# Another order for the opening of a paged-attention kernel: second tile's projections, key-head copies and one batch's values

## Chip, cores and metric

The kernel runs on one core of a Trainium2 chip. The metric is the time of one execution on the device in microseconds (us). The profile is of one further execution, taken by the hardware profiler. The core has five engines with an instruction stream each: TensorE (PE; its weight loads are shown apart as PEld), VectorE (DVE), ScalarE (ACT), GpSimd (POOL) and SyncE (SP), which here only issues transfers. An engine takes its instructions in order and waits at semaphores.

## What is computed

64 sequences of 32 tokens with 512 channels go through two residual layers, in float32. The first adds a 32 x 32 mix of the tokens that the sequence's condition picks. The second is grouped-query attention with 32 query and 8 key heads of 128 channels, over 512 cached positions (masked beyond the sequence's length) and the 32 new ones, with normed and rotated queries and keys, and an output projection.

```python
x = x + einsum('bct,bcd->bdt', x, weights[condition])
q = rope(rmsnorm(x @ Wq.T), pos)
k = rope(rmsnorm(x @ Wk.T), pos)
v = x @ Wv.T
k_all = concat(k_cache[block_table], k)
v_all = concat(v_cache[block_table], v)
o = softmax(mask(q @ k_all.T * scale)) @ v_all
x = x + o @ Wo.T
```

## The kernel before

**Tiles and steps.** Four sequences (batches, 4 x 32 = 128 tokens) make a tile; there are 16 tiles. Each is passed twice, once for each half of the key heads (four key heads, sixteen query heads), which gives 32 steps. A step has 16 slots: four batches by four score groups. A slot makes one group's scores and exponentials (`scores`, L1027 and L1038) and one earlier group's values (`values`, L1090, with its division on DVE, L1101 to L1104). Further work is put into slots by hand, among it the next tile's projections (`plan`, filled through `at`).

**A tile's input.** `x1_a` loads x. `x1_c` mixes tokens with one product against a block-diagonal matrix `bds` (L408) and adds on DVE (L409). `x1_b` transposes the result on PE (L416), and ACT copies it to `x1t` (L421). `q_a` and `k_a` project (L470, four products of 512 columns, eight rows in the trace), and `finish` squares on ACT (L479), takes the root on POOL (L487, L488), and norms and rotates on DVE (L496 to L514). The tile of the squares is also one of the rotation's two. `q_b` and `k_b` (`to_columns`) transpose the rows on PE (L527), and ACT copies them into `q_ring` (L612). PE's products for all of these share four PSUM banks in rotation ("pp").

**Cached keys and values.** `load_half` issues eight transfers of 64 KB on SP for half a batch's keys (`k_t`, three buffers); `head_keys` copies two heads of one half into `kh` (L1016 on ACT, L1018 on DVE; four buffers). For score group j the half is j // 2 and the heads are those of j % 2. `fetch` gathers 128 value rows with an indirect transfer from POOL (L354; three buffers) and `fill` copies them, masked, into `v_ring` (L366).

**The opening.** The first 130 lines or so of the main part (from `first, second = steps[0:2]`) are written out in the order in which each engine takes them, with no slots: the first tile's whole input, its projections, batch 0 and the beginning of batch 1, and of the second tile the mix and the key projection. In the list below, PE's order there, the second tile is marked with a 2:

mix, transposes, queries 0, keys, queries 1, queries 2, rows of queries 0 and keys, values of the new tokens, rows of queries 1, scores (0,0), mix 2, scores (0,2), values (0,0), queries 3, rows of queries 2, transposes 2, keys 2, rows of queries 3, scores (0,1), (0,3), new scores, scores (1,0), new values. Queries 0 to 3 of the second tile stand in slots 4 to 7 of step 0.

**SP's order there.** x, condition weights (`w_all`), query weights 0 and 1, keys of batch 0, value weights, x of tile 2, four blocks of condition weights for tile 2 (L288), query weights 3, keys of batch 1 (first half), the second half, six parts of the output weights (`wo`), keys of batch 2, x of tile 3, its four blocks, six more parts of `wo`, keys of batch 3, and so on. SP and ACT share eight semaphores for their transfers, so that an issue waits for the landing of an earlier transfer with its semaphore. Key weights and query weights 2 are issued by POOL.

**Sines.** Angles are reduced on DVE (`reduced`, seven operations) and their sines taken on ACT, for two tiles at a time; `rot_tables` makes a tile's rotation tables on POOL and DVE. A table load on ACT (L1278) readies the exponential.

## Time and profile before

| what | us |
|---|---|
| runs shown (3): lowest, median, highest | 2072.66, 2073.85, 2074.44 |
| profiled execution, its own time | 2073.99 |
| its span | 2072.1 |
| PE busy, of the span | 2044.2 |
| DVE busy | 1629.5 |
| POOL busy | 1002.9 |
| ACT busy | 958.4 |
| PE busy in the first 63 us | 52.60 |
| mean granted PE clock, whole span | 0.997 |

The span runs from the program's first instruction to its last; the execution's own time has 1.9 us more around it. Rows of the profile give an engine, a source line, the operation and the tiles it writes and reads (out<-in), the partitions by elements, how often, and the time; an idle time before is given with what ended it. An "L" with a number is a line of the kernel before.

### The profile page before, as it was taken

To read this page: it belongs to the slowest core of one execution; us is meant where nothing else is said; L and a number is where in the kernel's file an instruction comes from. 1 tells how busy PE (TensorE), PEld (TensorE's weight loads), DVE (VectorE), ACT (ScalarE), POOL (GpSimd) and SP (SyncE) were. 2 spreads that over 40 slices of the span, in tenths; PEclk is the share of its full clock that TensorE was granted. 3 is DMA by queue.
4 is the path that set the end of the run, shared out by engine and by line. 5 is a ranking of instruction groups with operands and counts; after the bars stand their busy time and mean duration, and the time that the engine had idled before them with its cause. 6 is when DMAs were issued, how large, how long until landed. Compare 5 with 4: busy or idle time off the path is not lost.

```text
span 2072.1 us, 45314 instructions
## 1 busy us (share of the span) xinstructions
PE 2044.2 (99%) x13460; PEld 1596.7 (77%) x13460; DVE 1629.5 (79%) x3533; ACT 958.4 (46%) x2707; POOL 1002.9 (48%) x1138
## 2 busy tenths in 40 slices
PE   8999999999999999999999999999999999999998
PEld 4767667787887878778786677878878788787897
DVE  4555687988969789697996769879797887979854
ACT  4444354444545444454434445344454445445351
POOL 4354465645636455363544445445363544536351
PEclk9999999999999999999999999999999999999999
DMA  8767557667676666787767876676767667676682
GB/s 244 198 183 223 154 153 233 184 196 217 180 219 191 210 201 189 212 265 223 217 190 208 233 207 195 196 206 180 213 182 216 185 193 210 184 211 180 191 233 75
DMA packets 410144, 413.33 MB, mean 199 GB/s; under 512 B 58944, under 2 KB 325824, under 8 KB 409888
## 3 DMA queue, kind: packets, MB, share of 16 engines
q1 hardware_dynamic: 353472, 228.55, 38.3%
q0 software_dynamic: 55680, 181.58, 28.7%
q8 instruction: 109, 1.79, 0.4%
q14 instruction: 147, 1.20, 0.2%
q10 hardware_dynamic: 736, 0.21, 0.0%
HBM read 350.09 MB, written 60.03 MB: 198 GB/s over the span
## 4 chain that ended last, share of the span: by engine, by line
PE 79%; DVE 7%; DMA 6%; SPq 3%; issue 3%; POOL 2%; ACT 1%; DVEq 0%; POOLq 0%; ACTq 0%
PE ps_x L1027 18%; PE po_x L1090 17%; PE p_x L837 13%; PE pb_x L698 8%; PE pc_x L698 6%; PE pa_x L698 5%; PE pout_x L794 3%; DMA k_t_x<-in_kt_dram 3%; SPq L321 2%; PE pnv_x L1072 2%; PE pp_q_x L470 2%; PE psn_x L1048 1%; DMA raw_x<-in_vc_dram,v_row 1%; PE pp_v_x L470 1%; DVE kh_x L1018 1%
## 5 line engine op out<-in xcount | busy, mean ns | idle before, releaser
L354 POOL DMA_INDIRECT raw_x<-in_vc_dram,v_row x512 | 550.7, 1076 | 626.7 <-ACT v_ring_x L366 513.2
L1038 ACT ACTIVATE pr_x<-ps_x 128x512 f32<-128x512 f32 x511 | 305.4, 598 | 777.5 <-PE ps_x L1027 772.4
L1090 PEld LDWEIGHTS po_x<-v_ring_x,pr_x 128*128 128x128 f32 x4088 | 523.5, 192 | 85.4 <-issue 67.3
L1027 PE MATMUL ps_x<-q_ring_x,kh_x 128*128 128x128 f32 x4088 | 547.7, 277 | 1.6 <-ACT q_ring_x L612 1.6
L1090 PE MATMUL po_x<-v_ring_x,pr_x 128*128 128x129 f32 x4088 | 544.1, 276 | 2.2 <-DVE nv_x L1101 2.2
L1027 PEld LDWEIGHTS ps_x<-q_ring_x,kh_x 128*128 128x128 f32 x4088 | 499.7, 192 | 13.9 <-issue 3.3
L366 ACT ACTIVATE v_ring_x<-raw_x,valid 128x512 f32<-128x512 f32 x512 | 342.9, 713 | 21.9 <-DMA raw_x<-in_vc_dram,v_row 21.5
L1018 DVE COPY kh_x<-k_t_x 128x512 f32<-128x512 f32 x506 | 218.6, 432 | 97.3 <-PE ps_x L1027 68.2
L544 POOL DMA_DIRECT2D heads_d<-rows_x x150 | 125.8, 839 | 278.0 <-DVE rows_x L540 211.1
L698 PE MATMUL pb_x<-t_x,early 128*128 128x512 f32 x504 | 238.4, 596 | 2.6 <-DVE t_x L726 1.2
L1101 DVE TENSOR_TENSOR nv_x<-po_x,nv_x 128x258 f32<-128x258 f32 x256 | 106.8, 417 | 101.3 <-PE po_x L1090 96.6
L837 PEld LDWEIGHTS p_x<-wo_x,ot_x 128*128 128x128 f32 x624 | 116.8, 190 | 62.1 <-issue 45.8
L488 POOL TENSOR_TENSOR rs_q_x<-ms_q_x,minus_half 128x4 f32<-128x4 f32 x128 | 158.7, 1240 | 10.7
L837 PE MATMUL p_x<-wo_x,ot_x 128*128 128x256 f32 x624 | 156.4, 380 | 0.1
L837 PE MATMUL p_x<-ts_x,ot_x 128*128 128x256 f32 x624 | 145.5, 380 | 0.0
L698 PEld LDWEIGHTS pb_x<-t_x,early 128*128 128x128 f32 x504 | 86.2, 191 | 65.4 <-issue 60.6
L837 PEld LDWEIGHTS p_x<-ts_x,ot_x 128*128 128x128 f32 x624 | 115.6, 191 | 24.2 <-issue 8.4
L1104 DVE TENSOR_TENSOR nv_x<-nv_x,rden 128x256 f32<-128x256 f32 x256 | 109.5, 428 | 8.7
L479 ACT ACTIVATE sq_q_x<-u_x 128x128 f32<-128x128 f32 x224 | 66.3, 298 | 93.9 <-DVE u_x L714 93.9
L698 PE MATMUL pc_x<-wq_x,early 128*128 128x512 f32 x224 | 105.4, 593 | 0.0
L698 PE MATMUL pa_x<-wq_x,early 128*128 128x512 f32 x224 | 105.4, 593 | 0.0
L514 DVE TENSOR_TENSOR rope_q_x<-rope_q_x,rs_q_x 128x512 f32<-128x512 f32 x120 | 82.2, 685 | 19.7 <-POOL rs_q_x L488 19.3
(207 smaller groups left out, 2629.6 us busy)
## 6 DMA issues: line engine op xcount, KB each, us to landing
k_t_x<-in_kt_dram SPq DMA_DIRECT2D x2048, 64.0 KB
heads_d<-rows_x POOLq DMA_DIRECT2D x150, 256.0 KB
q_ring_x<-heads_d SPq DMA_DIRECT2D x464, 80.0 KB
raw_x<-in_vc_dram,v_row POOLq DMA_INDIRECT x512
wo_x<-in_wo_dram SPq DMA_DIRECT2D x32, 256.0 KB
res_x<-acc_d SPq DMA_DIRECT2D x31, 256.0 KB
wq_x<-in_wq_dram SPq DMA_DIRECT2D x8, 512.0 KB
early<-x1t_d SPq DMA_DIRECT2D x16, 256.0 KB
```

Source lines behind the costliest of these rows:

```text
L354: nc.gpsimd.indirect_dma_start(out=raw.rearrange("p g d -> p (g d)"), out_offset=None, in_=vc, in_offset=bass.IndirectOffsetOnAxis(ap=v_ro ...
L366: nc.scalar.activation(v_ring[:, c, :, 0:D], raw, AF.Copy, scale=valid[:, b, c : c + 1])
L488: nc.gpsimd.tensor_tensor(rs, ms, minus_half, ALU.pow)
L544: nc.gpsimd.dma_start(heads_d[st.n][:, :, i, :].rearrange("k p c -> p k c"), part)
L698: nc.tensor.matmul(bank, pair.x[:, i, c, :], by[:, c * 512 : (c + 1) * 512], start=start and c == 0, stop=c == 1, skip_group_check=not start,)
L837: nc.tensor.matmul(to, left[:, i, :], right(i), start=start and i == 0, stop=i == QH // 2 - 1, skip_group_check=True,)
L1018: nc.vector.tensor_copy(to, src)
L1027: nc.tensor.matmul(ps[:, c, i, :], ba.k[j][:, i, c, :], queries(ba, g + i), start=True, stop=True,)
L1038: nc.scalar.activation(pr, ps, AF.Exp, scale=SCALE)
L1090: nc.tensor.matmul(ba.po[g][:, i, :], ba.pr[j][:, c, i, :], ba.v_t[:, 2 * half + c, g + i, :], start=(half == 0 and c == 0 and i == 0), st ...
L1101: nc.vector.tensor_tensor(t, ba.po[g], t, ALU.add)
L1104: nc.vector.tensor_tensor(t[:, :, 0:D], t[:, :, 0:D], rd.unsqueeze(2).to_broadcast([P, 2, D]), ALU.mult,)
```

## The change

In the opening:

- the second tile's x is loaded between query weights 0 and 1, and its block-diagonal matrix is filled from `w_all` by DVE, as the first tile's is, in place of four transfers;
- its mix stands behind the first query projection, its transposes behind the second, its tables and the write of its x behind the third; `x1t` of the second tile lies in another buffer ("acc") than the first's;
- its key projection and query projections 0 and 1 move: keys and queries 0 before the values of the new tokens, queries 1 behind the first tile's queries 3 (queries 0 and 1 were in slots 4 and 5);
- the angles and sines of tiles 2 and 3 come behind the second tile's key projection, with the exponential's table load, in another buffer ("nv");
- batch 0's key heads are copied in the order 0, 1, 2, 3: two behind the second tile's key projection, two behind its queries 0;
- the values of batch 0, group 0, stand behind the rows of the first tile's queries 3.

PE's order is then: mix, transposes, queries 0, mix 2, keys, queries 1, transposes 2, queries 2, rows of queries 0 and keys, keys 2, rows of queries 1, queries 0 of 2, values of the new tokens, scores (0,0), (0,2), queries 3, rows of queries 2, queries 1 of 2, rows of queries 3, values (0,0), scores (0,1), (0,3), new scores, scores (1,0), new values. SP no longer issues the four blocks; x of tile 2 comes earlier; the rest keeps its order.

```diff
@@ x1_b
             if st.pair is None:
+                tag = "x1t" if exact else "acc" if st.n == 1 else "u3"
...
+                    tag=tag,
+                    bufs=2 if tag == "acc" else 1,
@@ opening
         load_w("q", 0, 0)
+        x1_a(second)
         load_w("q", 0, 1)
...
         load_w("v", 0)
-        x1_a(second)
...
+        def pick_weights(t):
+            number = conditions(t, mybir.EngineType.DVE)
+            for i in range(BT):
+                blk = slice(i * S, (i + 1) * S)
+                nc.vector.tensor_copy(
+                    bds[t][blk, blk],
+                    w_all[:, bass.ds(number[i], 1), :].rearrange("p o e -> p (o e)"),
+                )
+
+        pick_weights(0)
...
-        load_cond_weights(1)
         load_w("q", 0, 3)
         later = Batch(first, 1)
         later.load_half()
+        pick_weights(1)
...
-        trig = work.tile([P, 3, TRIG * HD], F32, tag="w1", name="trig1", bufs=1)
-        reduced(TRIG, trig)
-        q_a(first, 0)
-        sines(new_trig(TRIG), trig)
-        table = small.tile([P, 1], F32, tag="rs", name="table")
-        nc.scalar.activation(table, half_pi, AF.Exp)
+        pp = project(first, wt["q", 0, 0], "pp_q_first")
+        x1_c(second)
+        finish(first, 0, pp, f"q_{first.name}_0", "q")
...
-        q_a(first, 1)
+        pp = project(first, wt["q", 0, 1], "pp_q_first_1")
+        x1_b(second)
+        finish(first, 1, pp, f"q_{first.name}_1", "q")
+        trig = work.tile([P, 3, TRIG * HD], F32, tag="nv", name="trig1", bufs=1)
         q_a(first, 2)
         fetch(0, RAW, tag="pn", bufs=1)
+        keep_x1(second, nc.gpsimd)
+        rot_tables(second)
         q_b(first, 0)
-        head_keys(batch, 0, nc.scalar)
-        head_keys(batch, 2, nc.scalar)
         k_b(first)
-        head_keys(batch, 1, nc.scalar)
+        k_a(second)
+        for j in (0, 1):
+            head_keys(batch, j, nc.scalar)
+        reduced(TRIG, trig)
+        q_b(first, 1)
+        q_a(second, 0)
+        for j in (2, 3):
+            head_keys(batch, j, nc.scalar)
+        sines(new_trig(TRIG), trig)
+        table = small.tile([P, 1], F32, tag="rs", name="table")
+        nc.scalar.activation(table, half_pi, AF.Exp)
         later.load_half()
-        head_keys(batch, 3, nc.scalar)
...
         new = v_product(first)
-        q_b(first, 1)
         scores(batch, 0)
...
         v_copy(first, new)
-        x1_c(second)
...
         scores(batch, 2)
-        values(batch, 0)
         q_a(first, 3)
         q_b(first, 2)
-        x1_b(second)
-        keep_x1(second, nc.gpsimd)
+        q_a(second, 1)
         head_keys(later, 0, nc.scalar)
         head_keys(later, 1, nc.scalar)
         after.load_half()
-        rot_tables(second)
-        k_a(second)
         q_b(first, 3)
+        values(batch, 0)
         scores(batch, 1)
@@ slots of step 0
-        for g in range(GH):
+        for g in (2, 3):
             at(0, 4 + g, lambda g=g: q_a(second, g))
```

## The prediction

> **What bounds the kernel now.** I read the busy table first, then TensorE's order of time over the opening, then the granted clock by stretch, and last SP's order of time with its waits and one row of DVE.
>
> ```profile
> PE 2044.2 (99%) x13460; PEld 1596.7 (77%) x13460; DVE 1629.5 (79%) x3533; ACT 958.4 (46%) x2707; POOL 1002.9 (48%) x1138
> ```
>
> TensorE (PE) is busy for all but 27.9 us of the 2072.1 us span. The change adds no matrix work and takes none away, so it can only win back idle time and slowly clocked time. The order of time of PE shows where the opening holds these (start, duration, engine, line, operation; in brackets the idle time before, and who ended it):
>
> ```profile
> 27.69 0.60 PE L527 MATMUL pt_x<-ident,rows_x 128*128 128x128 f32 x4
> 29.37 0.63 PE L527 MATMUL pt_x<-ident,rows_x 128*128 128x128 f32 x4 [1.07 <-DVE rows_x L514]
> 32.78 6.30 PE L470 MATMUL pp_v_x<-wv_x,x1t_x 128*128 128x512 f32 x8 [2.79 <-DMA wv_x<-in_wv_dram]
> ...
> 40.19 0.94 PE L1027 MATMUL ps_x<-q_ring_x,kh_x 128*128 128x128 f32 x6 [0.45 <-ACT q_ring_x L612]
> ...
> 43.61 3.60 PE L470 MATMUL pp_q_x<-wq_x,x1t_x 128*128 128x512 f32 x8
> ...
> 49.54 3.70 PE L470 MATMUL pp_k_x<-wk_x,x1t_x 128*128 128x512 f32 x8 [1.45 <-ACT x1t_x L421]
> ...
> 55.08 0.94 PE L1027 MATMUL ps_x<-q_ring_x,kh_x 128*128 128x128 f32 x6 [1.18 <-ACT q_ring_x L612]
> ```
>
> Five waits: 1.07 + 2.79 + 0.45 + 1.45 + 1.18 = 6.94 us. The value projection also takes 6.30 us where the same eight matmuls take 3.60 us at 43.61. The windows say why (columns: stretch, PE, PEld, DVE, ACT, POOL busy, granted clock, DMA share, GB/s):
>
> ```profile
> 30.00:35.00 5.00, 2.22 (x3) 1.18 (x4) 3.58 (x8) 3.09 (x13) 4.58 (x6) 0.62 0.96 287
> 35.00:40.00 5.00, 4.74 (x12) 2.00 (x10) 1.69 (x4) 1.53 (x4) 1.12 (x1) 0.69 0.91 311
> 40.00:45.00 5.00, 4.81 (x28) 3.62 (x29) 0.83 (x2) 3.98 (x8) 1.92 (x2) 1.00 0.47 134
> ```
>
> The clock is halved from 31.25 to 38.08 us, after the wait for wv: 2.70 us lost. The ceiling of the change is thus 6.94 + 2.70 = 9.64 us.
>
> The second stream to watch is SP's, which issues the keys (k_t), the output weights (wo) and more, in one order:
>
> ```profile
> 24.75 0.51 SPq L264 DMA_DIRECT2D wv_x<-in_wv_dram  x1
> ...
> 43.94 3.30 SPq L262 DMA_DIRECT2D wo_x<-in_wo_dram  x6
> 48.52 15.49 SPq L321 DMA_DIRECT2D k_t_x<-in_kt_dram  x16
> ...
> 66.95 2.89 SPq L262 DMA_DIRECT2D wo_x<-in_wo_dram  x6
> ```
> ```profile
> SPq L321 <- DMA wo_x<-in_wo_dram: 10.1, 11, 1.9
> ```
> ```profile
> 95.17 0.43 DVE L1018 COPY kh_x<-k_t_x 128x512 f32<-128x512 f32 x1 [1.76 <-DMA k_t_x<-in_kt_dram]
> ```
>
> The second fence is from SP's wait list of 36 to 115 us (total, times, longest): key issues stood 10.1 us behind landings of wo, 11 times. The third is from DVE's order of time: at 93.41 it wanted the keys of batch 4 and waited 1.76 us. Nobody on PE felt it, but the keys were no longer early there.
>
> **The change, part by part.** Times of the changed kernel are estimates: its order of instructions, filled with the durations above.
>
> *Loads.* The second tile's x (256 KB) goes ahead of the second query weights; its four weight blocks (SP busy from 26.43 to 29.32) become four DVE copies from w_all. The same step for the first tile took 0.73 us for four copies, after at most 0.9 us for reading the numbers; DVE stands idle for 2.63 us at that place, until 13.48 (lens), so 1.6 us is hidden. Without that cover it would be 1.6 us. 256 KB more at the 380 GB/s of 10 to 16 us is 0.7 us on the queue: query weights 1 land at 20.9 instead of 20.22 (5.19 + 15.03 in the chain of waits), PE wants them at 21.7; each later key issue, and wv, go 0.7 us later (wv lands near 33.3; 24.75 + 7.89 in that chain before), and wq3, issued at 29.37 before, goes out near 26.3.
>
> *Mixing the second tile behind the first projection.* PE: 0.86 us; DVE's sum comes at 20.0, when the masks are done, where `reduced(TRIG)` (2.07 us, at 19.87) stood. That and the two sines and the table load on ACT no longer hold the first rope back: it starts at 20.75 instead of 23.00. From there ropes and squares alternate over one buffer (squares at 25.17, rope at 26.35, squares at 28.54): 3.36 us for each projection.
>
> *Key and query projection of the second tile before the value projection.* PE runs on without a wait: projection 13.73 to 17.39, mix 18.25, keys 21.70, queries-1 25.14, transposes 25.57, queries-2 29.0, two transposes 29.86, second tile's keys 33.3, one transpose 33.75, its queries-0 37.2, values 40.64 (wv is there since 33.3). 1.07, 2.79 and the slow clock are gone.
>
> *What comes next is late instead.* POOL has the second tile's tables (six operations, 1.69 us) behind the fourth fetch and the acc write: they end at 36.4. So the second key rope starts at 36.1, `reduced` ends at 41.05, the sines at 42.05, the table load (1.28) and its use at 43.55; behind these in ACT's order stands the first exponential (41.17 before). Then exponential, four fills, value copy, exponential (4.0 us, as 41.17 to 45.19) and the squares of queries-3: 47.65 to 48.8. Rope and rows end at 51.7, and PE, which has finished the second tile's queries-1 at 49.7, waits 2.05 us for them. After 0.45 + 0.85 + 0.39 us of work it waits another 0.5 us for the last query columns, behind two key copies on ACT. The scores that ran at 55.08 run at 53.95.
>
> *Key heads.* The order 0, 1, 2, 3 puts the copies at 34.9 to 36.1 and 39.4 to 40.6, against 33.39 to 36.08 before: later, not earlier. What it costs is the buffers' release; SP does not want the first before 37.4 nor the second before 46, so nothing.
>
> *Values of batch 0 behind the fourth query group.* 0.89 us that now fills part of that wait; no cost.
>
> *Slots 4 and 5.* Two projections less, 2 x 3.44 = 6.88 us. With 55.08 - 53.95 = 1.13 us, PE stands 8.0 us ahead there.
>
> *The cover that went.* The 6.88 us lay over the key loads. SP's stream does not gain 8 us: it hangs on landings. It is ahead by what wq3 does: key issues resume near 37.4 instead of 38.31, a further gain from the acc write leaving the wo stretch (256 KB, at some 200 GB/s 1.3 us), and a loss from two value fetches that now fall into the second wo stretch (0 to 2.6 us). I take 1.5 us; bounds 0 and 3.0. DVE takes batch 4's keys in order, and behind them the queue to the third tile's sum: from 95.17 to 103.98, less 2.42 us of waits for PE, is 6.4 us. So the transposes of L416, at 104.85 before, could have run at 101.7: the slack is 3.1 us. The gain there is 3.1 + 1.5 = 4.6 us, not 8.0 (bounds 3.1 and 6.1). Past 130 us SP waits for DVE again, and what is won stays.
>
> **Sum.** min(8.0, 4.6) = 4.6 us off the profiled execution's 2073.99 us: 2069.4; against the median 2073.85: 2069.25 us.
>
> *Rule against row.* The new 2.05 us wait lies in a 3.41 us window with 1.4 us of work in it, 41%; before, the clock fell after a window that PE filled to 32%, and, near 1168 us, to 64% with many 32-row products. So I count up to 1.7 us (one window at half clock) against PE's 8.0, which leaves 6.3 and does not touch the 4.6.
> The Trainium skill (TensorE: Matmul & The Clock Gate, "Part 1: The HAM clock gate") asks for an idle window of about 3.4 us before the clock drops; the trace disagrees, since 2.79 us of waiting was enough. By the rule PE would keep its 8.0 us.
>
> **Rivals.**
>
> *PE's path decides (22%).* SP keeps pace, since its keys are never late for PE itself in the profile. Gain 8.0, or 6.3 with the slow clock: 2065.9 to 2067.6. Against it: DVE's 1.76 us wait.
>
> *Keys not earlier at all, fetches in the way (15%).* Stream 1.1 us late (2.6 - 1.5): gain 2.0 us, 2071.9. For it: 66 to 80 us has a DMA share near 1 in the windows.
>
> *Slower (13%): slow clock in the thinned slots.* Without the two projections PE waits for keys in slots 8 to 15. Where more than 2.3 us of a 3.41 us window is waited, the clock halves as at 31.25 and costs 3.4 us (6.83 us at half). Two such falls on top of the former rival: 2.0 - 6.8 = 4.8 us lost, 2078.6. Against it: before, PE filled 67% of its worst window there (85.9 to 89.3) at full clock.
>
> *The change doesn't do what it says* holds for the key heads: they are not copied as they land. It costs nothing above, so it moves no number.
>
> **How the numbers follow.** Forecast 50% (2067.7 to 2070.8 from its bounds), rivals 22, 15 and 13. A measurement here can tell some 0.2%, 4.15 us, from no change: below 2069.7 is faster. Of the forecast's range about six tenths lie below that: 0.30 + 0.22 = 0.52 faster; 0.20 + 0.15 = 0.35 the same; 0.13 slower. The range for 8 in 10 goes from 2065.4 (PE's path) to 2073.5 (keys without gain, plus one window at half clock).
>
> **What would show it.** Right: no wait before pp_v and clock 1.00 from 14 us to 48; a PE wait of about 2 us on the fourth queries' rows near 50; a DVE wait for k_t of 5 us or more between 84 and 95, and PE's idle behind it. Wrong: no such DVE wait (then 8 us), or a wait of PE in the opening's first 40 us (wq1, wv or the ropes late), or PEclk below 1 between 80 and 105 us.

## The result and the profile after

The changed kernel takes 2069.15 us in the median of 22 runs (2064.80 to 2077.22), the kernel before 2074.18 us in as many on the same chips. The ratio is 0.9981, its 95% interval 0.9973 to 0.9989: 3.9 us less, somewhere from 2.3 to 5.6 (the medians alone lie 5.0 us apart). The profiled span is 2068.4 us against 2072.1.

From the page of the changed kernel, the busy times:

```profile
PE 2043.8 (99%) x13460; PEld 1596.8 (77%) x13460; DVE 1633.0 (79%) x3537; ACT 954.7 (46%) x2707; POOL 1003.6 (49%) x1138
```

TensorE idles for 24.6 us where it idled for 27.9, and its busy time is 0.4 us shorter. That nearly the same work was done with less waiting is all that these two numbers say; where the waits went, TensorE's order of time shows (start, duration, engine, line, operation, tiles; in brackets the idle time before and who ended it; lines are those of the changed kernel, where L470, L527, L1027 and L1090 have become L475, L532, L1032 and L1095):

```profile
36.34 3.60 PE L475 MATMUL pp_v_x<-wv_x,x1t_x 128*128 128x512 f32 x8
...
50.96 0.63 PE L532 MATMUL pt_x<-ident,rows_x 128*128 128x128 f32 x4 [1.92 <-DVE rows_x L519]
...
79.72 1.13 PE L1095 MATMUL po_x<-v_ring_x,pr_x 128*128 128x129 f32 x8 [2.56 <-DVE nv_x L1106]
80.69 1.80 PE L1032 MATMUL ps_x<-q_ring_x,kh_x 128*128 128x128 f32 x8
82.28 1.93 PE L1095 MATMUL po_x<-v_ring_x,pr_x 128*128 128x129 f32 x8
...
98.62 0.60 PE L416 MATMUL px1t_x<-ident,acc_x 128*128 128x128 f32 x4
```

The wait for wv is gone and the value projection takes 3.60 us (6.30 before). The opening's five waits are gone; a new one of 1.92 us, for the rows of the fourth queries, has come. And in slot 9 of the first step the wait is longer: 2.56 us at 79.72, where the kernel before waited 1.13 us at 87.58. The two groups behind it take 1.80 and 1.93 us where such a group takes 1.06. The kernel before, in the same order of time:

```profile
87.58 1.13 PE L1090 MATMUL po_x<-v_ring_x,pr_x 128*128 128x129 f32 x8 [1.13 <-DVE nv_x L1101]
...
104.85 0.60 PE L416 MATMUL px1t_x<-ident,acc_x 128*128 128x128 f32 x4
```

The windows of the changed kernel's profile (stretch, busy PE, PEld, DVE, ACT, POOL, granted clock, DMA share, GB/s) give the reason:

```profile
76.00:79.40 3.40, 1.16 (x11) 0.97 (x9) 2.94 (x7) 2.45 (x6) 2.92 (x4) 1.00 0.90 238
79.40:82.80 3.40, 3.08 (x19) 3.11 (x20) 2.78 (x10) 0.28 (x2) 1.78 (x2) 0.71 0.80 235
82.80:86.20 3.40, 3.40 (x26) 3.40 (x26) 2.07 (x6) 1.32 (x3) 0.00 (x0) 0.79 0.75 212
```

After the thin window the clock is half for 3.4 us, from 80.8 to 84.2. What TensorE waits for stands on DVE behind two rotations, these behind ScalarE's squares, and these behind a fill, in ScalarE's order of time:

```profile
63.62 0.75 ACT L366 ACTIVATE v_ring_x<-raw_x,valid 128x512 f32<-128x512 f32 x1
70.48 0.72 ACT L366 ACTIVATE v_ring_x<-raw_x,valid 128x512 f32<-128x512 f32 x1 [6.11 <-DMA raw_x<-in_vc_dram,v_row]
...
71.59 0.27 ACT L484 ACTIVATE sq_q_x<-pp_q_x 128x128 f32<-128x128 f32 x1
```

The projection whose squares start at 71.59 had ended on TensorE at 68.4: ScalarE stood still for 6.11 us at the fill ahead of them, whose gather had not landed. In the kernel before the same fill waited for nothing. GpSimd's issue of its gather there and, below it, in the changed kernel:

```profile
65.18 1.10 POOL L354 DMA_INDIRECT raw_x<-in_vc_dram,v_row  x1 [9.19 <-ACT v_ring_x L366]
```
```profile
62.95 1.31 POOL L354 DMA_INDIRECT raw_x<-in_vc_dram,v_row  x1 [10.24 <-ACT v_ring_x L366]
```

ScalarE's order of time in the kernel before:

```profile
67.38 0.28 ACT L479 ACTIVATE sq_q_x<-pp_q_x 128x128 f32<-128x128 f32 x1 [1.88 <-PE pp_q_x L470]
...
69.58 1.32 ACT L366 ACTIVATE v_ring_x<-raw_x,valid 128x512 f32<-128x512 f32 x2
```

There the squares of the projection in slot 4 stand ahead, and ScalarE comes to the fill, the second of that pair, near 70.2, some 5.0 us behind the issue of its gather. In the changed kernel it comes to it at 70.48 - 6.11 = 64.37, 1.4 us behind the issue.

And the keys, which the prediction takes for the limit? SP's order of time:

```profile
41.97 2.80 SPq L262 DMA_DIRECT2D wo_x<-in_wo_dram  x6
46.34 11.27 SPq L321 DMA_DIRECT2D k_t_x<-in_kt_dram  x16
57.79 0.34 SPq L396 DMA_DIRECT2D acc_x<-in_x_dram  x1
```

In this execution the third tile's x goes out at 57.79 us (64.13 before), and DVE's copies of keys never wait for a landing between 45 and 150 us.

A measure that a time of 2070 us with some 3 us of scatter (the standard deviation of the changed kernel's 22 runs is 3.3) can't drown is the **stretch** from the start of the first projection to the transposes of the third tile's mixed x (L416): 104.85 - 13.73 = 91.12 us before, 98.62 - 12.59 = 86.03 us after, 5.1 us less. To the fourth tile's transposes it is 158.25 and 153.47 us, 4.8 us less; to the end of the span it is 2072.1 - 13.73 = 2058.4 and 2068.4 - 12.59 = 2055.8 us, only 2.6 us less. The start of the first projection is left out of it: it lies at 13.73 us before and between 11.7 and 12.9 us in all later profiles, b1_loads among them; whether that belongs to the change was not tried.

### The profile page after: what moved, and what is told of

Read it like the earlier page. It is cut to its first block, busy times and chain, and to the rows that moved or that the text cites. A ratio compares the mean times of both kernels' runs of the same rounds, so it can differ in the third digit from the quotient of the medians.

```text
span 2068.4 us, 45310 instructions
## 1 busy us (share of the span) xinstructions
PE 2043.8 (99%) x13460; PEld 1596.8 (77%) x13460; DVE 1633.0 (79%) x3537; ACT 954.7 (46%) x2707; POOL 1003.6 (49%) x1138
## 4 chain that ended last, share of the span: by engine, by line
PE 77%; DVE 8%; DMA 4%; issue 3%; SPq 3%; POOL 2%; ACT 2%; DVEq 0%; ACTq 0%; POOLq 0%
PE po_x L1095 18%; PE ps_x L1032 18%; PE p_x L842 13%; PE pb_x L703 8%; PE pc_x L703 6%; PE pa_x L703 5%; PE pout_x L799 3%; DMA k_t_x<-in_kt_dram 2%; SPq L321 2%; PE pnv_x L1077 2%; DMA raw_x<-in_vc_dram,v_row 1%; PE pp_q_x L475 1%; PE psn_x L1053 1%; DVE kh_x L1023 1%; POOL rs_q_x L493 1%
## 5 line engine op out<-in xcount | busy, mean ns | idle before, releaser
L1095 PEld LDWEIGHTS po_x<-v_ring_x,pr_x 128*128 128x128 f32 x4088 | 524.6, 192 | 87.0 <-issue 70.0
L1095 PE MATMUL po_x<-v_ring_x,pr_x 128*128 128x129 f32 x4088 | 546.0, 276 | 3.9 <-DVE nv_x L1106 3.2
L1032 PE MATMUL ps_x<-q_ring_x,kh_x 128*128 128x128 f32 x4088 | 548.1, 277 | 0.2
L1032 PEld LDWEIGHTS ps_x<-q_ring_x,kh_x 128*128 128x128 f32 x4088 | 500.4, 192 | 12.6 <-issue 3.3
L842 PEld LDWEIGHTS p_x<-ts_x,ot_x 128*128 128x128 f32 x624 | 115.4, 190 | 24.6 <-issue 8.4
```

What stands on the lines that cost most here:

```text
L842: nc.tensor.matmul(to, left[:, i, :], right(i), start=start and i == 0, stop=i == QH // 2 - 1, skip_group_check=True,)
L1032: nc.tensor.matmul(ps[:, c, i, :], ba.k[j][:, i, c, :], queries(ba, g + i), start=True, stop=True,)
L1095: nc.tensor.matmul(ba.po[g][:, i, :], ba.pr[j][:, c, i, :], ba.v_t[:, 2 * half + c, g + i, :], start=(half == 0 and c == 0 and i == 0), st ...
```

## The experiments

All start from the changed kernel, except b1_loads. "Lead" is by how much sooner than before SP issues the third tile's x, counted from the first projection (64.13 - 13.73 = 50.40 us before). Ratios are to the kernel before.

| kernel | ratio, 95% interval | stretch, us | TensorE's wait in slot 9 | its wait for the third tile's sum | lead |
|---|---|---|---|---|---|
| before | 1 | 91.12 | 1.13 | none | 0 |
| changed | 0.9981 (0.9973, 0.9989) | 86.03 | 2.56 | none | 5.2 |
| a0_again | 0.9986 (0.9972, 1.0000) | 86.16 | 3.22 | 0.1 | 2.4 |
| e1_fill_late | 0.9983 (0.9969, 0.9997) | 86.12 | 3.37 | none | 3.1 |
| e2_wo_late | 0.9973 (0.9962, 0.9985) | 84.79 | 1.14 | 0.98 | 2.4 |
| e3_warm | 0.9975 (0.9962, 0.9987) | 85.30 | filled | none | 3.4 |
| e4_v_first | 1.0005 (0.9991, 1.0018) | 92.84 | 2.80 | none | -1.4 |
| e5_acc_late | 0.9976 (0.9962, 0.9989) | 88.28 | 2.80 | 2.23 | 1.9 |
| e6_values_back | 0.9987 (0.9976, 0.9999) | 88.27 | 2.65 | none | 4.3 |
| e7_heads_back | 0.9982 (0.9968, 0.9995) | 88.85 | 4.07 | none | 1.4 |
| e9_fills_behind | 0.9974 (0.9961, 0.9987) | 86.03 | 1.22 | 2.96 | 2.4 |
| e10_both | 0.9952 (0.9936, 0.9967) | 84.87 | 1.22 | none | 1.5 |
| e11_filled | 0.9963 (0.9949, 0.9977) | 84.44 | 1.21 | none | 1.1 |
| b1_loads | 0.9993 (0.9978, 1.0007) | 89.86 | 1.14 | none | 2.1 |

By time only e4 and e10 stand apart from the changed kernel; the other intervals overlap with its own, and there the profiles decide.

**a0_again: the changed kernel, profiled once more.**

> The changed kernel itself, profiled a second time. Question: how much of what its first profile shows is one execution's luck. In that profile the third tile's x was issued at 57.79 us, behind 11.27 us for 16 key issues; two of its variants with the same order of loads up to there took 13.75 and 13.58 us and issued it at 59.7. Theory 'the stream of loads differs by some 2 us from execution to execution': here it is issued at 58 to 61 us, ScalarE's wait for the gather of batch 1, chunk 3, lies anywhere from 2.5 to 6.5 us, and DVE may wait for the keys of batch 4 by up to 3.5 us without TensorE feeling it. Theory 'the variants are slower streams': x at 57.5 to 58.1 and no wait of DVE for keys. Both: TensorE's waits up to 60 us after its first projection are those of the first profile within 0.5 us, the stretch from the first projection to the third tile's transposes is 85 to 88.5 us.

The stream of loads does differ that much. SP's order of time:

```profile
46.54 14.07 SPq L321 DMA_DIRECT2D k_t_x<-in_kt_dram  x16
60.80 0.34 SPq L396 DMA_DIRECT2D acc_x<-in_x_dram  x1
```

DVE's:

```profile
85.82 0.43 DVE L1023 COPY kh_x<-k_t_x 128x512 f32<-128x512 f32 x1 [3.29 <-DMA x1t_d<-x1t_x]
...
92.29 0.43 DVE L1023 COPY kh_x<-k_t_x 128x512 f32<-128x512 f32 x1 [3.33 <-DMA k_t_x<-in_kt_dram]
...
96.56 0.43 DVE L1023 COPY kh_x<-k_t_x 128x512 f32<-128x512 f32 x1 [0.49 <-DMA k_t_x<-in_kt_dram]
...
98.23 0.68 DVE L409 TENSOR_TENSOR acc_x<-pmix_x,acc_x 128x512 f32<-128x512 f32 x1
```

Same program, 2.8 us less lead, and now DVE waits 7.1 us in three places before copies of keys, more than the 3.5 us allowed for. (The bracket of the first names a write of x1t; transfers share semaphores, so the name can be another transfer's. The copy reads a `k_t` tile, and in e9_fills_behind the wait at the same place is put down to `k_t`.) The sum at 98.23 ends at 98.91, and TensorE takes the transposes at 98.96, having worked to 98.82. So both limits, TensorE's stall in slot 9 (3.22 us, half clock behind it) and the keys, end within 0.1 us of each other in this execution.

**e1_fill_late and e9_fills_behind: fills behind the squares.** First the one fill that waited 6.11 us:

```diff
-                        for _ in unfilled[:2]:
+                        for _ in unfilled[: 1 if st.n == 0 and slot == 5 else 2]:
                             next_values()
...
+        at(0, 6, lambda: next_values())
```

> The changed kernel, with one thing moved: in slot 5 of the first step ScalarE fills one chunk of cached values instead of two, and the second fill (batch 1, chunk 3) follows the squares of the second tile's third query projection, in slot 6. In the changed kernel's profile this fill waited 6.11 us for its gather, the squares stood behind it, and TensorE then waited 2.56 us and ran 3.4 us at half clock. Measure: from the start of the first projection to the transposes of the third tile's mixed x, 91.12 us in the kernel before and 86.03 us in the changed one. Theory 'the order on ScalarE costs it': the first rope behind it starts near 69.6 instead of 72.75 us, TensorE's wait of 2.56 us falls under 1 us, the clock stays at 1.00 between 76 and 90 us, and the stretch is 82.8 to 84 us (2 to 3.2 us less); the kernel's time 2066 to 2067 us. Rival 'the keys limit' (the prediction's): the stretch stays at 86 us within 0.5, since DVE then waits for keys instead. Rival 'the gather limits': values of chunk 3 come too late for TensorE in slot 7, which waits there for the fill; the stretch is within 1 us of 86.

The first squares did come early, at 67.59, but the stretch stayed at 86.12. ScalarE's order of time:

```profile
72.48 0.72 ACT L366 ACTIVATE v_ring_x<-raw_x,valid 128x512 f32<-128x512 f32 x1 [2.50 <-DMA raw_x<-in_vc_dram,v_row]
74.53 0.72 ACT L366 ACTIVATE v_ring_x<-raw_x,valid 128x512 f32<-128x512 f32 x1 [1.32 <-DMA raw_x<-in_vc_dram,v_row]
75.15 0.26 ACT L484 ACTIVATE sq_q_x<-pp_q_x 128x128 f32<-128x128 f32 x1
```

The next two fills, with gathers late in their turn, stood ahead of the next projection's squares (ended on TensorE at 72.7, squared from 75.15). The theory named too few fills. So the second kernel put those behind the squares too:

```diff
-        for g in (2, 3):
-            at(0, 4 + g, lambda g=g: q_a(second, g))
+        at(0, 6, lambda: q_a(second, 2), lambda: next_values())
+        at(0, 7, lambda: q_a(second, 3), lambda: next_values(), lambda: next_values())
...
-                    if g % 2:
+                    if g % 2 and (st.n or slot not in (5, 7)):
                         for _ in unfilled[:2]:
                             next_values()
+                    elif g % 2 and slot == 5:
+                        next_values()
```

> The changed kernel, with ScalarE's fills of cached values in slots 5 and 7 of the first step behind the squares of the second tile's third and fourth query projections (one fill stays in slot 5, one goes to slot 6, two of slot 7 go behind the squares). Moving the first alone left the stall: the fourth projection's squares then stood behind two later fills, each late for its gather. Theory 'the order of fills and squares on ScalarE sets the stall': squares of the fourth query projection start within 0.8 us of its end, its rope some 2 us earlier against the first projection than in the changed kernel (63.5 us behind it, in both profiles of it), TensorE's wait near 67 us behind it falls from 2.56 and 3.22 us to 0.6 to 1.3, the clock stays at 1.00 there. What the stretch from the first projection to the third tile's transposes then does tells the second limit: 'TensorE alone' gives 82.8 to 84 us (86.03 and 86.16 in the changed kernel), 'the keys are the next limit' gives 84.5 to 86.5 with a wait of TensorE for DVE's sum of the third tile and waits of DVE for keys before it. Rival 'gathers come too late for the values themselves': TensorE waits for a fill instead, and nothing is won.

TensorE's order of time and, below it, DVE's:

```profile
78.05 1.13 PE L1095 MATMUL po_x<-v_ring_x,pr_x 128*128 128x129 f32 x8 [1.22 <-DVE nv_x L1106]
...
98.71 0.66 PE L416 MATMUL px1t_x<-ident,acc_x 128*128 128x128 f32 x4 [2.96 <-DVE acc_x L409]
```

```profile
85.93 0.43 DVE L1023 COPY kh_x<-k_t_x 128x512 f32<-128x512 f32 x1 [5.06 <-DMA k_t_x<-in_kt_dram]
...
91.54 0.43 DVE L1023 COPY kh_x<-k_t_x 128x512 f32<-128x512 f32 x1 [2.59 <-DMA k_t_x<-in_kt_dram]
...
96.30 0.43 DVE L1023 COPY kh_x<-k_t_x 128x512 f32<-128x512 f32 x1 [0.98 <-DMA k_t_x<-in_kt_dram]
97.97 0.68 DVE L409 TENSOR_TENSOR acc_x<-pmix_x,acc_x 128x512 f32<-128x512 f32 x1
```

This is the decisive pair. The stall in slot 9 is down to 1.22 us, no half clock follows it, and TensorE is ready for the third tile at 98.71 - 2.96 = 95.75, that is 83.07 us behind its first projection. There it waits 2.96 us for a sum that DVE makes late, after 8.6 us of waits for keys. The stretch is 86.03 again: with the first limit taken away, the second holds the same place. (Behind it e9 does worse: the fourth tile's transposes come at 154.81 us, 153.47 in the changed kernel.) The first limit is the order of fills and squares on ScalarE, the second the keys.

**e2_wo_late: three parts of the output weights later.** They stood ahead of the keys of batches 3 and 4, in time beside three gathers.

```diff
-        for part in (3, 4, 5):
-            load_parts(outputs, 0, part)
+        for j in range(3):
+            later_of(0, 9 + j, lambda j=j: load_parts(outputs, 0, 3 + j))
```

> The changed kernel, with the loads of output weight parts 3, 4 and 5 (1.5 MB in all, issued at 60.58 to 63.4 us there) moved into slots 9, 10 and 11 of the first step. Theory 'the gather was late because these loads were in its way': the gather of batch 1, chunk 3, issued near 63 us, lands some 4 us later instead of 7.5, so ScalarE's wait of 6.11 us shrinks to 3 or less; TensorE's wait near 79.7 us is under 1.2 us, no half clock follows, and the stretch from the first projection to the third tile's transposes is 82.8 to 84 us (86.03 in the changed kernel). If the loads only move the trouble, a later fill or DVE's key copies wait behind them in slots 9 to 14, and the stretch is 85 to 87. Theory 'the gather is slow by itself': the 6.11 us stay within 1 us, and so does the stretch.

ScalarE's fills and TensorE's two waits:

```profile
66.90 0.72 ACT L366 ACTIVATE v_ring_x<-raw_x,valid 128x512 f32<-128x512 f32 x1 [2.73 <-DMA raw_x<-in_vc_dram,v_row]
...
70.54 1.32 ACT L366 ACTIVATE v_ring_x<-raw_x,valid 128x512 f32<-128x512 f32 x2
```

```profile
78.09 1.13 PE L1095 MATMUL po_x<-v_ring_x,pr_x 128*128 128x129 f32 x8 [1.14 <-DVE nv_x L1106]
...
96.51 0.66 PE L416 MATMUL px1t_x<-ident,acc_x 128*128 128x128 f32 x4 [0.98 <-DVE acc_x L409]
```

The next two fills found their gathers landed; with the weights beside them they waited 1.59 and 2.08 us in a0_again, 2.50 and 1.32 in e1. The stall and the half clock are gone. But the moved parts, issued at 80.67 and 89.44, now stand between keys, DVE waits 2.10 and 2.47 us, and TensorE 0.98 us. (The brackets of both name `wo`; as in a0_again, the copies read `k_t`, and the name can be another transfer's.) The stretch, 84.79, lies between the two bands expected. The first theory holds for the gathers and the "trouble moves" clause for the keys; the fourth tile's transposes come at 153.25 us, no better than the changed kernel's 153.47.

**e3_warm: the wait in slot 9 filled with idle products.**

```diff
+        later_of(0, 9, lambda: keep_warm(20))
```

> The changed kernel, with 20 matrix products of 128x128 whose result nobody reads, put into slot 9 of the first step, just ahead of the values for which TensorE waited 2.56 us there (in the profile, 79.72 us). It measures the price of the half clock that follows by itself: the wait is filled and TensorE stays busy. Theory 'the low clock costs 1.6 us, the wait itself is not shortened by it': the products take 1.8 to 2.4 us, the rest of the wait is under 0.8, the clock stays at 1.00 between 76 and 90 us, and the stretch from first projection to third tile's transposes is 84 to 84.8 us (86.03 before it). Rival 'something else sets the third tile's mix': the clock stays up but the stretch does not fall under 85.5, and TensorE waits later instead.

```profile
76.24 4.63 PE L1253 MATMUL warm<-ident 128*128 128x128 f32 x40
```

That row of TensorE's order of time is the filler: 20 products are 40 rows and take 4.63 us, twice what was expected, more than the wait. The clock stays up, and the stretch falls to 85.30 all the same, 0.7 to 0.9 us less, short of the 84 to 84.8 expected. By this one profile the half clock cost at least that; its full size isn't separated, since the filler itself took too long.

**e4_v_first: the value projection back ahead of the second tile's projections.**

```diff
         k_b(first)
+        new = v_product(first)
         k_a(second)
...
-        new = v_product(first)
         scores(batch, 0)
```

> The changed kernel, with the value projection of the first tile back ahead of the second tile's key projection and first query projection, which in the changed kernel lie over the wait for its weights. Prediction's step: TensorE comes to the value projection near 29 us, wv lands near 33, so it waits some 3 to 4 us and half a clock window to two of them follow (2.7 us before the change): the stretch from the first projection to the third tile's transposes is 90 to 92.5 us (86.03 in the changed kernel, 91.12 in the kernel before), the kernel's time 4 to 6 us above the changed one. Rival 'the cover is not what wins, the other edits are' (earlier mix, earlier ropes): the stretch stays within 1.5 us of 86. Rival 'there is slack behind': the loss in the opening is taken back by shorter waits at 51 and 79 us, and the stretch is 87 to 88.5.

In TensorE's order of time the wait for wv is back, and a half clock behind it:

```profile
31.78 5.37 PE L475 MATMUL pp_v_x<-wv_x,x1t_x 128*128 128x512 f32 x8 [2.69 <-DMA wv_x<-in_wv_dram]
```

The stretch is 92.84, above the expected band and above the kernel before; the median 2076.14 us against 2074.07. Nothing behind takes the loss back: the later waits stay (2.51 and 2.80 us), and SP falls behind too. Without these two projections over the wait for wv nothing of the gain is left: the expected 4 to 6 us above the changed kernel is what the ratios give (1.0005 and 0.9981, 5 us apart).

**e5_acc_late, e7_heads_back, b1_loads: where SP's lead comes from.** The first puts the write of the second tile's x back to near 50 us, the second copies the key heads in the old order, the third gives the kernel before the new loads alone.

```diff
-        keep_x1(second, nc.gpsimd)
         rot_tables(second)
...
         q_b(first, 2)
+        keep_x1(second, nc.gpsimd)
```

> The changed kernel, with the write of the second tile's mixed x to memory (256 KB, issued by GpSimd at 33.55 us there) back to where the kernel before has it, behind the columns of the third query group (near 50 us, between the key loads and the output weights). Open question: why SP's stream of keys ran 6 to 9 us ahead of the kernel before, where the prediction gave it 1.5. Theory 'the write was in the way of the output weights': SP's waits for output weights go from 3.1 us back to 8 or more, the 16 key issues behind 46.3 us take 14 us or more (11.27 in the changed kernel, 15.49 before), and the third tile's x is issued at 61 us or later (57.79; 64.13 before). Theory 'the stream follows what releases its buffers and what was issued ahead of it': these move by less than 1.5 us. In both the stretch from first projection to third tile's transposes stays near 86 us if the keys do not limit, and grows by 2 us or more if they do.

```diff
-        for j in (0, 1):
-            head_keys(batch, j, nc.scalar)
+        head_keys(batch, 0, nc.scalar)
+        head_keys(batch, 2, nc.scalar)
...
-        for j in (2, 3):
-            head_keys(batch, j, nc.scalar)
+        head_keys(batch, 1, nc.scalar)
...
         later.load_half()
+        head_keys(batch, 3, nc.scalar)
```

> The changed kernel, with the key heads of batch 0 copied in the order and at the places relative to the loads of the kernel before (0 and 2 first, then 1, then 3 behind the load of the second half of batch 1). Prediction's step: the order of these copies costs and wins nothing, because SP wants their buffers later than they come free: the key issues start within 0.7 us of the changed kernel's (41.97 for the first output weights, 46.34 for the next 16 keys), and the stretch stays within 1 us. Rival 'it frees the key buffers earlier and that is why SP ran ahead': the output weights are issued 1 us or more later than 41.97, and the third tile's x at 61 us or later.

```diff
         load_w("q", 0, 0)
+        x1_a(second)
         load_w("q", 0, 1)
...
-        x1_a(second)
...
-        load_cond_weights(1)
...
         later.load_half()
+        pick_weights(1)
```

> The kernel before, with the change's loads alone: the second tile's x ahead of the second query weights, and its four weight blocks copied by DVE from the weights already there instead of loaded by SP (2.89 us of SP's time). It asks how much of SP's lead comes from these two. Prediction's step: the DVE copies are hidden, 1.6 us under the wait for the lengths, and SP's stream is about 1 us ahead from this. Theory 'the loads give half of the lead or more': the first output weights are issued at 41.5 to 42.8 us (43.94 in the kernel before; 41.97 and 42.45 in the changed one), the third tile's x at 61 to 63 us (64.13; 57.79 and 60.80). Rival 'the projections' order gives the lead, since it frees buffers earlier': 43.5 or later, and 63.5 or later. In both TensorE's waits before 60 us stay those of the kernel before within 1.5 us in sum, the wait for wv (2.79 us) among them, so the stretch from the first projection to the third tile's transposes is 89.5 to 92 us (91.12), and the kernel's time within 1.5 us of the kernel before.

Seven profiles of kernels whose program is the same up to the third tile's x (the changed one twice, e1, e2, e3, e9, e10) have leads of 1.5 to 5.2 us, 2.9 in the mean. The loads alone (b1) give 2.1 us, but not in the same place. They issue the first output weights 28.70 us behind the first projection (30.21 before), 1.5 us sooner, and gain 0.55 us from there to the third tile's x (19.64 us, 20.19 before). In the seven profiles it is the other way round: the output weights come 0.4 us sooner in the mean (0.8 later to 1.3 sooner), and the rest of the lead, 1.8 to 4.4 us, arises behind them. What shortens that part no run separates: it is as short with the write back (e5, 18.24 us), with the key heads back (e7, 18.33) and with the value projection back (e4, 17.28). The loads also win 1.26 us of stretch, since wv comes sooner (a wait of 1.70 us) and one half-clock window replaces two, though the time doesn't tell b1 from the kernel before (0.9978 to 1.0007); the DVE copies that replace SP's loads cost nothing that is seen.

With the write back (e5) the lead is 1.9 us, within that spread, and SP's waits for output weights are 10.9 us, where the changed kernel has 3.1 in one profile and 10.0 in the other: whether the write was in the way stays open. But e5 is the second sight of the keys as the limit, in TensorE's order of time:

```profile
100.96 1.03 PE L416 MATMUL px1t_x<-ident,acc_x 128*128 128x128 f32 x4 [2.23 <-DVE acc_x L409]
```

With the key heads in the old order (e7) SP issues the output weights 30.69 us behind the first projection, and the seven have 28.88 to 31.01; its lead of 1.4 us lies just below theirs. An effect of the order doesn't stand out on SP. The stretch of 88.85, well outside the expected 1 us, comes from a longer stall in slot 9 (4.07 us, two windows at half clock), behind three fills that waited 2.65, 1.92 and 2.60 us; whether the order of the copies has a part in it one profile can't say, and the times don't tell the two kernels apart.

**e6_values_back: the values of batch 0 at their old place.**

```diff
         scores(batch, 2)
+        values(batch, 0)
         q_a(first, 3)
...
         q_b(first, 3)
-        values(batch, 0)
```

> The changed kernel, with the first values of batch 0 back behind the scores of its third head group, as in the kernel before. Prediction's step: moving them costs nothing and wins at most what they fill. With them back, TensorE comes to the transposes of the fourth queries 0.89 us later, so its wait there falls from 1.92 to about 1.0 us, and it waits 0.6 to 1.1 us for the columns behind them (none in the changed kernel): the stretch from first projection to third tile's transposes moves by less than 0.7 us either way. Rival 'the move is a gain of its own': a new wait of more than 1.5 us, or a half clock near 51 us, and 1.5 us or more lost.

TensorE's order of time:

```profile
43.74 1.32 PE L1095 MATMUL po_x<-v_ring_x,pr_x 128*128 128x129 f32 x8 [2.15 <-ACT v_ring_x L366]
...
55.25 0.94 PE L1032 MATMUL ps_x<-q_ring_x,kh_x 128*128 128x128 f32 x6 [1.67 <-ACT q_ring_x L617]
```

A wait of 2.15 us at the old place, because the fills now come later on ScalarE (behind sines, table load and exponential), and 1.67 us for the columns that the values had covered; the wait for the fourth rows falls to 0.36. The stretch is 2.1 to 2.2 us longer: by this profile the move was needed and the rival is right, while the times (0.9987 and 0.9981) don't tell.

**e10_both and e11_filled: both limits away.** e10 is e9 with output weight parts 3, 4 and 5 in slot 15 of the first step and slots 1 and 3 of the second; e11 adds a filler to the wait for the fourth rows.

```diff
-        for part in (3, 4, 5):
-            load_parts(outputs, 0, part)
+        for j, slot in enumerate(((0, 15), (1, 1), (1, 3))):
+            later_of(*slot, lambda j=j: load_parts(outputs, 0, 3 + j))
```

> The changed kernel, with both: the fills of slots 5 to 7 behind the squares as in e9_fills_behind, and output weight parts 3, 4 and 5 loaded in slot 15 of the first step and slots 1 and 3 of the second, behind the third tile's mix, instead of ahead of the key loads of batches 3 and 4. Theory 'two limits lie side by side, the squares' chain and the keys': with both gone the stretch from the first projection to the third tile's transposes is 82.5 to 84 us, with no half clock near 68 us behind the first projection, no wait of TensorE for the third tile's sum and under 1.5 us of waits of DVE for keys of batch 4; what is won stays at 150 us behind the first projection (150.5 to 151.5 against 153.47 in both profiles of the changed kernel) unless the moved loads hold up the second step; the kernel's time is 2 to 3 us under the changed one's. Rival 'a third limit': the stretch stays over 84.5 us. Rival 'the loads only move the trouble': the stretch falls, and the gain is gone by 150 us.

```diff
         q_a(second, 1)
+        keep_warm(14)
         head_keys(later, 0, nc.scalar)
```

> The kernel e10_both, with 14 matrix products of 128x128 whose result nobody reads between the second tile's second query projection and the transposes of the fourth query group, where TensorE waits 1.5 to 2.2 us for rows. In the profile of e10_both this wait (2.18 us, in a window of 3.4 us that TensorE filled to 38%) was followed by one window at half clock, in the eight other profiles with the change's order of work there it was not (waits of 1.55 to 2.13 us). The products take 1.6 us (0.116 us each in e3_warm). Theory 'that window is what e10_both lost': no half clock near 38 us behind the first projection, the rest of the wait under 0.7 us, the transposes of the fourth query group no later than 39 us behind the first projection, the stretch from there to the third tile's transposes 82.8 to 83.7 us (84.87 in e10_both), and 150 to 151 us where 153.47 stands for the changed kernel; the time is that of e10_both or up to 1.5 us less. Rival 'the clock is not the price': the stretch stays at 84.5 to 85.2 without a half clock, since something else sets the third tile's mix.

In e10 no wait of TensorE for the sum is left, DVE's copies of batch 4's keys wait 0.3 us at most, and the stretch is 84.87, out of its band for a reason that the windows show:

```profile
47.40:50.80 3.40, 1.30 (x4) 0.23 (x2) 2.74 (x5) 1.65 (x11) 1.79 (x3) 1.00 1.06 222
50.80:54.20 3.40, 3.32 (x16) 3.35 (x17) 2.74 (x5) 1.91 (x7) 1.26 (x2) 0.50 1.05 229
```

The wait for the fourth rows, 2.18 us here, let the clock fall. From those rows to slot 9 TensorE worked 27.39 us (50.88 to 79.49, less 1.22 of waiting), in e9 26.20 (50.63 to 78.05, less 1.22): 1.2 us. In e11 the clock stays up, but the filler took 3.29 us instead of the 1.6 expected, so the fourth rows' transposes come at 39.99 us behind the first projection (38.67 in e10; no later than 39 was expected) and the stretch is 84.44, again out of its band. From the fourth rows to the third tile's transposes e11 takes 44.45 us and e10 46.20, so the half clock was a price of e10. To the fourth tile's transposes it is 152.06 and 151.57 us (153.47): some 1.4 and 1.9 us are kept. 2065.79 and 2065.26 us in the median (8 and 6 runs, on different chips) are 10.5 and 8.6 us under the kernel before on the same chips; e10's interval lies wholly below the changed kernel's, e11's touches it. That is more than their stretch explains (6.3 and 6.7 us). Neither profile has the half-clock window near 1160 us that the kernel before and the changed one's first profile have; the rest is open.

## Why the prediction was right, and where it wasn't

**The time.** Forecast 2069.25 us, measured 2069.15. That the two agree to 0.1 us is luck: the gain was forecast at 4.6 us, and the ratio leaves anything from 2.3 to 5.6. The stretch fell by 5.1 and 5.0 us where the forecast had 4.6. "What is won stays" is seen only as far as the fourth tile (4.8 us in both profiles). From the first projection to the end of the span both profiles of the changed kernel are no more than 2.6 and 2.5 us shorter than the kernel before's one. In the variants the part behind the fourth tile moves by several us either way (e1 ends 7.5 us ahead of the kernel before, e3 1.5 us behind it), and no run takes it apart.

**Both terms of min(8.0, 4.6) are seen in e9**, the kernel with its fills moved, not in the changed kernel itself: TensorE ready 91.12 - 83.07 = 8.05 us sooner (forecast 8.0), held by keys to 91.12 - 86.03 = 5.1 us (forecast 4.6). Mis-sized was the stream's lead, 1.5 us in the forecast, 2.9 in the mean of seven profiles and 2.4 in e9. Its own terms (0.9 us from wq3, 1.3 from the write, a loss of 0 to 2.6) come to -0.4 to 2.2, so 1.5 and the upper bound of 3.0 were a choice rather than a sum. No run shows the 1.3 us of the write as a gain of its own, and where the lead arises is only in part the loads' doing (b1). The slack, taken as 3.1, comes out at 5.1 - 2.4 = 2.7 in e9.

**The opening is as forecast.** No wait over 0.2 us from 14 to 48 us in either profile of the changed kernel, wv covered (e4: a stretch 6.8 us longer when it isn't), 1.92 and 1.55 us for the fourth rows (forecast 2.05). The second pair of new values starts 46.88 us behind the first projection (47.98 before), 1.10 us sooner against a forecast of 1.13.

**The step that failed is "The cover that went".** It saw only key loads under the two projections that left slots 4 and 5. They had also lain over the chain of gather, fill, squares, rotation and division in slots 5 to 9. Without them ScalarE comes to the fourth fill of batch 1 1.4 us behind the issue of its gather instead of 5.0, and every instruction behind the fill waits with it. That made TensorE's wait in slot 9 2.56 and 3.22 us instead of 1.13, with a window at half clock behind it. In the first profile this is 1.4 us more of waiting and 1.6 us for the two slow groups (1.80 + 1.93 against 2 x 1.06), which takes TensorE's own lead from 8.05 (e9) to 5.1 us. That the order of fills and squares makes the stall, e9 shows, and that the output weights beside the gathers have a part in it, e2; that the two projections had covered it before is read from the two traces, and no run put them back. By two of the prediction's own signs, no wait of DVE for keys and a clock under 1 between 80 and 105 us, this part of its path was wrong in the first profile. That the time was right all the same is luck: in the first profile the stall alone decides (no wait for keys), in the second the stall and the keys end within 0.1 us of each other, and nothing in the prediction makes the two meet.

**The waits at which it would show.** Five us or more of waits of DVE for keys between 84 and 95: none in the first profile, 6.6 between 82 and 93 in the second, 7.7 in e9. TensorE's idle behind it: 0.1 us in the second, 2.96 in e9.

**Values at no cost, key heads at no cost.** The first was too low: e6's profile puts the move at 2 us of stretch, since the old place would have waited for fills that the new sines push back. The second stays open: on SP no effect is clear of the spread.

**The clock.** The prediction kept the full clock as a loss of at most 1.7 us for the window near 50 us. It stayed up in both profiles of the changed kernel there, and fell in e10 after 2.18 us, for 1.2 us; the section on the hardware shows why. The Trainium skill (TensorE: Matmul & The Clock Gate, "Part 1: The HAM clock gate") has windows of about 3.4 us that run on by themselves, which the traces bear out, and asks for an idle one before the clock drops, which they contradict: in e10 the window was 38% busy.

**Rivals.** "PE's path decides" is half right: TensorE did decide in the first profile, but with 5.1 us, not 8.0. "Fetches in the way" named a real collision (e2), felt by the gathers rather than the keys. The slower case did not come, though its half clock did, once.

## What to carry to other kernels

Before work is moved out of a stretch, list every chain that it lay over there, not only the transfer that was last seen late: an in-order engine that takes copies of gathered data ahead of other work hands each late gather on to everything behind it. When one limit is taken away and the time doesn't move, look for a second wait at the same meeting point before the theory is dropped; only e9's wait of 2.96 us, not its time, told the two apart. And profile the same kernel twice before a difference of 2 to 3 us in a stream of transfers is explained.

## What the runs showed of the hardware

The clock falls by a fixed grid, not by the length of a wait. In every profile that has more than one, the starts of the half-clock windows lie whole multiples of 3.41 us apart, over up to 600 of them ((1162.8 - 80.8) / 317 = 3.413 in the changed kernel). Laying that grid over TensorE's idle time from 20 to 180 us in thirteen profiles (e11 has no half clock there and but one later), every full-clock window with 2.06 us or more of idle time was followed by one at half clock (13 of 13), and none with 1.80 us or less was. So the 2.51 us wait of e4 passed, because a border of the grid cut it (1.52 and 1.12 us with what lay beside it), and the 1.70 us wait of b1 did not, because part of a wait of 0.99 us lay in the same window (2.28 together). Where a border falls differs from execution to execution: the wait of some 2 us for the fourth rows is safe in one and costs 1.2 us in another.

Idle time is not the whole measure, though. Near 1160 us, and once near 1220, seven windows in six profiles were followed by half clock with only 0.90 to 1.54 us of idle time in them (1.22 us, or 64% busy, in the kernel before, at 1164.5 to 1167.9). In all seven, products of 32 rows (`pnv`) take 0.65 to 1.53 us of the window; whether these count for less was not tried.

The same gather, issued near 62.5 us, had its fill start 4.1 us after issue in e2 (62.75 to 66.90), 4.9 in a0_again (62.46 to 67.33) and 7.5 in the first profile (62.95 to 70.48). The same 16 key issues took from 11.27 to 14.07 us in two executions of one program.
